# Layer 0's scores and values as 64x64 quadrant matmuls in turns, and one scatter with each step

## The chip, the cores and the metric

The kernel runs on one core of a Trainium2 chip. The metric is the device time of the whole program in microseconds (us); the kernel before takes 2517.85 us (median of 3 runs, 2517.65 to 2518.61). Times of single instructions come from one profiled execution of the same program, which took 2627.8 us.

## What is computed

Eight images of 256 channels and 1024 pixels go through two layers, all in fp32. Only layer 0 is touched by the larger part of the change, and the dispatch of layer 1's experts by the smaller part:

```python
# layer 0, per image: 8 heads of 64
qkv  = xt @ w_qkv + b_qkv
attn = softmax(einsum('bihd,bjhd->bijh', q, k) * 64**-0.5, axis=1)   # over the queries i
res  = einsum('bijh,bjhd->bihd', attn, v) @ w_out + b_out + xt
# layer 1, per image
t = t + attention(layer_norm(t))              # one head of width 256
t = t + moe(layer_norm(t))                    # 8 experts, the best 2 of each token
```

The softmax of layer 0 runs over the queries, so the sum that a score is divided by belongs to a key. The kernel folds it into the values.

## The kernel before, in words

The images go through `layer0` (L369), `attend` (L518), `normed` (L684) one after the other. Of seven images the tokens are scattered by expert to a table in DRAM (`dispatch`, L697), and one pass of `experts` (L867) works on them all; the eighth image goes through `dense`.

In `layer0` the heads are taken in pairs g (four pairs) and the keys in blocks j of 128 (eight blocks), so there are 32 steps (g, j) for an image and 256 in all. The queries and keys of a head pair lie as two times 64 partitions in `q` and `k`. One step does this:

- `score(at, h, n)` (L384): for head h = 0 or 1 and half n of the 1024 queries, a matmul with 64 rows (the width of a head) and 128 columns (the keys of the block), 512 queries long: psc. Head 0 uses the upper 64 rows of the array and head 1 the lower 64, so two of them can run at once. A score tile psc of one head fills two PSUM banks, and three such tiles exist (`ps_big`).
- `first_max` (L397) and `soften` (L406): VectorE takes the largest score of the first half (L401), then of the second half together with the first (L413); ScalarE writes the exponentials `ex` and their sum (L423); VectorE divides the values by the sum (L430, L432): `vs`.
- `gather_values(at)` (L439), which lags two steps behind (`LAG`): for each half n of the queries and each head h, a matmul with all 128 rows (the keys) and 64 columns (the width of the head), 512 queries long, added up in `po[n]` over the eight blocks. Head 0 uses columns 0 to 63 and head 1 columns 64 to 127, so again two can run at once.

The loop at L461 writes the order down by hand: score (at, head 0, first half), score (at-1, head 1, second half), `soften` of head 1, score (at, head 0, second half), score (at, head 1, first half), `soften` of head 0, and then the values of step at-2. In two steps of each of the first three head pairs a projection of the next pair follows (`project`, L292; 4 matmuls on the full array: pqk). With each step the generator `routing`, which is `dispatch` of the image before, is moved on to its next `yield` (L489). `dispatch` has 16 such places; behind the last of them it issues all 16 scatters (8 token blocks by 2 choices, L763) at one go. The tile framework's scheduler then places the instructions in five queues, one for each engine, and joins them by semaphores.

A matmul in fp32 is two instructions here, so the profile counts twice as many as the code writes; this text calls each of the two a pass.

Of the kernel before, what the change touches and what calls it, by code (L numbers as in the profile page):

```python
# [11 lines left out]
I32 = mybir.dt.int32  # L12
AF = mybir.ActivationFunctionType
ALU = mybir.AluOpType
AX = mybir.AxisListType


@with_exitstack
def kernel(
# [23 lines left out]
    nc = tc.nc  # L43
    P = 128
# [3 lines left out]
    DK = 64  # L48
    SCALE = DK ** (-0.5)
    NCC = C // P  # L50
    NT = S // P
    NH2 = S // 512
# [15 lines left out]
    small = ctx.enter_context(tc.tile_pool(name="small", bufs=6))  # L68
# [300 lines left out]
    def layer0(b, xT, begun, routing):  # L369

        v, qks = begun.v, begun.qks
        array = None
        res = one.tile([P, NPAIR, S], F32, tag="res", name=f"res_{b}")
        steps = [(g, j) for g in range(NPAIR) for j in range(NT)]
        LAG = 2
        seconds = {}  # L380
        pss, firsts, nmaxes, exps, sums, vss = {}, {}, {}, {}, {}, {}
        po = None

        def score(at, h, n):  # L384
            g, j = steps[at]
            q, k = qks[g]
            if n == 0:
                pss[at, h] = big(f"psc_{b}_{g}_{j}_{h}")
            r = slice(h * DK, (h + 1) * DK)
            mm = nc.tensor.matmul(  # L390
                pss[at, h][:, ts(n, 512)], k[r, ts(j, P)], q[r, ts(n, 512)], start=True, stop=True
            )
            if n == 1:

                tc.declare_no_dep(mm.ins, firsts.pop((at, h)).ins, reason="the other bank")

        def first_max(at, h):  # L397

            g, j = steps[at]
            nmax = small.tile([P, 1], F32, tag="nmax1", name=f"nmax1_{b}_{g}_{j}_{h}")  # L400
            firsts[at, h] = nc.vector.tensor_reduce(  # L401
                nmax, pss[at, h][:, ts(0, 512)], AX.X, ALU.max, negate=True
            )
            nmaxes[at, h] = nmax

        def soften(at, h):  # L406

            g, j = steps[at]
            ps = pss.pop((at, h))
            if h == 0:  # L410
                sums[at] = small.tile([P, 2], F32, tag="sums", name=f"sums_{b}_{g}_{j}")
            nmax = small.tile([P, 1], F32, tag="nmax", name=f"nmax_{b}_{g}_{j}_{h}")
            seconds[h] = nc.vector.tensor_scalar(  # L413
                scrap,
                ps[:, ts(1, 512)],
                -1.0,
                nmaxes.pop((at, h)),
                ALU.mult,
                ALU.min,
                accum_out=nmax,  # L420
            )
            ex = expp.tile([P, 1024], F32, tag="exps", name=f"ex_{b}_{g}_{j}_{h}")
            nc.scalar.activation(  # L423
                ex, ps, AF.Exp, bias=nmax, scale=1.0, accum_out=sums[at][:, h : h + 1]
            )
            exps[at, h] = ex
            if h == 1:

                rs = small.tile([P, 2], F32, tag="rs", name=f"rs_{b}_{g}_{j}")
                nc.vector.reciprocal(rs, sums.pop(at))  # L430
                vs = four.tile([P, 2, DK], F32, tag="vs", name=f"vs_{b}_{g}_{j}")
                nc.vector.tensor_mul(  # L432
                    vs,
                    v[:, j, ts(g, P)].rearrange("p (h d) -> p h d", d=DK),
                    rs.unsqueeze(2).to_broadcast([P, 2, DK]),
                )
                vss[at] = vs

        def gather_values(at):  # L439
            nonlocal po  # L440
            g, j = steps[at]
            if j == 0:
                po = [acc(f"po_{b}_{g}_{n}") for n in range(NH2)]
            vs = vss.pop(at)
            exs = [exps.pop((at, h)) for h in range(2)]
            for n in range(NH2):
                for h in range(2):
                    mm = nc.tensor.matmul(  # L448
                        po[n][h * DK : (h + 1) * DK, :],
                        vs[:, h, :],  # L450
                        exs[h][:, ts(n, 512)],
                        start=(j == 0),
                        stop=(j == NT - 1),
                    )
            if j == NT - 1:
                for n in range(NH2):
                    nc.scalar.copy(res[:, g, ts(n, 512)], po[n])
            return mm

        last = len(steps) - 1  # L460
        for at in range(last + LAG + 1):  # L461
            if at <= last:
                score(at, 0, 0)
            if 0 < at <= last + 1:
                score(at - 1, 1, 1)
                soften(at - 1, 1)
            if at <= last:

                with tc.issue_after(seconds[1].ins) if 1 in seconds else nullcontext():
                    first_max(at, 0)  # L470
                score(at, 0, 1)
                score(at, 1, 0)
                soften(at, 0)
                with tc.issue_after(seconds[0].ins):
                    first_max(at, 1)
            if at == 0:
                begun.rest()
                next(routing, None)
            if at >= LAG:
                array = gather_values(at - LAG)  # L480
            if at <= last:
                g, j = steps[at]
                if g + 1 < NPAIR and j in (3, 5):
                    if j == 3:
                        qks.append([])
                    qks[g + 1].append(project(b, xT, g + 1, len(qks[g + 1])))
                if array is not None:
                    with tc.issue_after(firsts[at, 1].ins), tc.issue_after(array.ins):
                        next(routing, None)  # L489
        for _ in routing:  # L490
            pass


        t1 = one.tile([P, NT, C], F32, tag="t1", name=f"t1_{b}")
        n = 1024 // C
        for i in range(0, NT, n):
            pt = big(f"pt_x_{b}_{i}")
            for j in range(n):
                for cc in range(NCC):
                    nc.tensor.transpose(  # L500
                        pt[:, j * C + cc * P : j * C + (cc + 1) * P], xT[:, cc, ts(i + j, P)], ident
                    )
            nc.vector.tensor_add(
                t1[:, i : i + n, :],
                pt.rearrange("p (j c) -> p j c", c=C),
                b_o.unsqueeze(1).to_broadcast([P, n, C]),
            )
        for i in range(NT):
            pr = acc(f"pr_{b}_{i}")
            for g in range(NPAIR):  # L510
                nc.tensor.matmul(  # L511
                    pr[:, :C], res[:, g, ts(i, P)], wo[:, g, :], start=(g == 0), stop=(g == NPAIR - 1)
                )
            nc.vector.tensor_add(t1[:, i, :], pr[:, :C], t1[:, i, :])
        return t1
# [181 lines left out]
    def dispatch(b, n2, l, group):  # L697

        gate, hots = yield from gates(b, l)
# [40 lines left out]
        group.counts = counts  # L740

        kept = []
        for k in range(2):
            yield
            hot = hots[k]
            sel = tmp("d_sel")
            nc.vector.tensor_mul(sel, hot, rows)
            row = keep.tile([P, NT], F32, tag=f"row{k}", name=f"row{k}_{b}")
            nc.vector.tensor_reduce(row, sel, AX.X, ALU.add)
            nc.vector.tensor_mul(sel, hot, e_iota.unsqueeze(1).to_broadcast([P, NT, E]))  # L750
            exp = keep.tile([P, NT], F32, tag=f"exp{k}", name=f"exp{k}_{b}")
            nc.vector.tensor_reduce(exp, sel, AX.X, ALU.add)
            yield
            to = small.tile([P, NT], F32, tag="d_to", name=f"d_to_{b}_{k}", bufs=2)
            nc.vector.scalar_tensor_tensor(to, exp, float(group.cap), row, ALU.mult, ALU.add)
            at = small.tile([P, NT], I32, tag="d_at", name=f"d_at_{b}_{k}", bufs=2)
            nc.vector.tensor_copy(at, to)  # L757
            kept.append((row, exp, at))
        for i in range(NT):
            for k in range(2):  # L760
                at = kept[k][2]
                view = group.views[2 * (NT * group.items.index(b) + i) + k]
                nc.gpsimd.indirect_dma_start(  # L763
                    out=view[:, :],
                    out_offset=bass.IndirectOffsetOnAxis(ap=at[:, i : i + 1], axis=0),
                    in_=n2[:, i, :],
                    in_offset=None,
                )
        group.kept[b] = gate, [(row, exp) for row, exp, _ in kept]

    def plan(group):

# [443 lines left out]
```

## Time and profile before

| what | value | where it is read |
|---|---|---|
| device time | 2517.85 us | the times |
| profiled execution | 2627.8 us, clock 0.979 | span and granted clock of the core |
| score passes psc (L390) | 2048, 553.3 us busy | groups of instructions |
| value passes po (L448) | 2048, 495.9 us busy | groups of instructions |
| VectorE per step: L413 and L401, two each | 750 and 679 ns | groups of instructions |
| ScalarE per step: L423, two | 1114 ns | groups of instructions |
| scatters (L763) | 112, 975 ns each on GpSimd | groups of instructions |

Busy time of PE counts a stretch once even where several passes run in it, so 2048 passes of mean 622 ns make 553.3 us. The chain that ended last is followed back from the last instruction; a share of it is time in which that line held up the end. `PE L390 <- ACT L423` after an idle time says that the matmul queue went on when that ScalarE instruction was done.

### The profile page before, as it was taken

Reading aid. Unit: us, or ns where it says so; the run is one execution under the profiler, and the core shown is the slowest. Engines: PE = TensorE matmul, PEld = TensorE weight load, DVE = VectorE, ACT = ScalarE, POOL = GpSimd, SP = SyncE. Lnnn points to the kernel's source line nnn. Section 1 sums busy time; section 2 is a strip of 40 time slices with the busy share of each in tenths; the row PEclk is TensorE's granted clock in tenths of the full one; section 3 lists DMA queues with packets and bytes.
Section 4 is the critical chain, followed back from the end, with each engine's and each line's share of the span. In section 5 each row is a group of like instructions: output and inputs, shape, how many; then the busy total and the mean of one; then the engine's idle time right before and its main releaser. Section 6 shows DMA issues by size and latency. Waiting matters only on the chain.

```text
span 2627.8 us, 27548 instructions
## 1 busy us (share of the span) xinstructions
PE 2504.9 (95%) x9919; PEld 1311.3 (50%) x9919; DVE 1538.1 (59%) x3738; ACT 891.0 (34%) x1491; POOL 386.0 (15%) x383
## 2 busy tenths in 40 slices
PE   9999989998999989998999899989998999997798
PEld 3346434643365336532563256324643488884566
DVE  5764766466656765576557664766476753334443
ACT  3541345134512542244214431444144422221212
POOL 0000020002000100002000200020002144435561
PEclk9999999999999999999999999999999999998899
DMA  7991000000000000000000000000000156663352
GB/s 289 385 333 44 32 33 17 1 17 33 1 17 17 19 15 17 16 1 33 17 17 1 32 17 0 17 32 1 0 17 33 53 196 225 214 196 100 104 166 103
DMA packets 82513, 187.61 MB, mean 71 GB/s; under 512 B 13992, under 2 KB 23880, under 8 KB 80584
## 3 DMA queue, kind: packets, MB, share of 16 engines
q1 hardware_dynamic: 57368, 118.65, 12.6%
q0 software_dynamic: 25008, 67.20, 8.2%
q8 instruction: 78, 1.28, 0.2%
q14 instruction: 59, 0.48, 0.1%
HBM read 100.49 MB, written 110.90 MB: 80 GB/s over the span
## 4 chain that ended last, share of the span: by engine, by line
PE 88%; DVE 3%; another core or an unknown queue 3%; issue 2%; DMA 2%; ACT 2%; SPq 0%; ACTq 0%; POOL 0%; DVEq 0%; POOLq 0%
PE psc L390 19%; PE po L448 17%; PE pqk L299 9%; PE py L571 8%; PE ps L545 7%; PE pr L511 4%; PE pv L335 4%; PE ph L903 3%; PE pe L928 3%; PE pdy L1110 2%; PE pdh L1086 2%; PE px L530 2%; PE pa L564 2%; PE pt_n L232 1%
## 5 line engine op out<-in xcount | busy, mean ns | idle before, releaser
L423 ACT ACTIVATE ex<-psc,nmax 128x1024 f32<-128x1024 f32 x512 | 570.5, 1114 | 639.5 <-DVE scrap L413 576.2
L390 PE MATMUL psc<-qk,qk 64*128 64x512 f32 x2048 | 553.3, 622 | 12.6 <-ACT ex L423 8.1
L413 DVE TENSOR_SCALAR_CACHE_REDUCE scrap<-psc,nmax 128x512 f32<-128x512 f32 x512 | 384.2, 750 | 229.7 <-PE psc L390 137.4
L448 PE MATMUL po<-ex,vs 128*64 128x512 f32 x2048 | 495.9, 605 | 2.1 <-DVE nmax L401 2.1
L390 PEld LDWEIGHTS psc<-qk,qk 64*128 64x128 f32 x2048 | 209.8, 185 | 337.7 <-ACT ex L423 176.1
L401 DVE TENSOR_REDUCE nmax<-psc 128x1 f32<-128x512 f32 x512 | 347.4, 679 | 16.6 <-PE psc L390 16.0
L299 PE MATMUL pqk<-xT,wqkv 128*128 128x512 f32 x512 | 249.8, 633 | 53.8 <-ACT ex L423 53.8
L448 PEld LDWEIGHTS po<-ex,vs 128*64 128x64 f32 x2048 | 124.8, 136 | 337.7 <-issue 212.5
L571 PE MATMUL py<-n,aT 128*128 128x256 f32 x1024 | 244.4, 393 | 16.7 <-DVE aT L566 11.9
L571 PEld LDWEIGHTS py<-n,aT 128*128 128x128 f32 x1024 | 196.0, 195 | 81.9 <-DVE aT L566 49.7
L545 PE MATMUL ps<-nT,xa 128*128 128x512 f32 x512 | 236.5, 592 | 0.0
L692 POOL TENSOR_TENSOR t<-t,n 128x2048 f32<-128x2048 f32 x8 | 36.3, 4537 | 1280.2 <-issue 1004.4
L299 PEld LDWEIGHTS pqk<-xT,wqkv 128*128 128x128 f32 x512 | 99.1, 201 | 195.8 <-issue 102.6
L763 POOL DMA_INDIRECT rows<-n,d_at x112 | 109.2, 975 | 593.3 <-DVE d_at L757 561.3
L556 ACT ACTIVATE ex<-ps,nmax 128x1024 f32<-128x1024 f32 x64 | 71.3, 1115 | 352.2 <-DVE nmax L553 321.9
L576 DVE SCALAR_TENSOR_TENSOR t<-py,rs,t 128x256 f32<-128x256 f32 x64 | 31.0, 484 | 232.6 <-PE py L571 201.7
L289 DVE TENSOR_SCALAR qk<-pqk,b_qk 128x512 f32<-128x512 f32 x100 | 75.1, 751 | 121.4 <-PE pqk L299 121.4
L545 PEld LDWEIGHTS ps<-nT,xa 128*128 128x128 f32 x512 | 93.6, 190 | 79.9 <-issue 73.7
L975 POOL DMA_INDIRECT yk<-y,yat x112 | 112.4, 1003 | 122.1 <-DVE o L1007 71.8
L335 PE MATMUL pv<-wqkv,xT 128*128 128x512 f32 x256 | 119.6, 596 | 1.0 <-ACT wqkv L105 1.0
L553 DVE TENSOR_REDUCE nmax<-ps 128x1 f32<-128x1024 f32 x64 | 78.3, 1224 | 59.1 <-PE ps L545 54.1
L511 PE MATMUL pr<-wo,res 128*128 128x256 f32 x512 | 111.8, 379 | 0.0
(191 smaller groups left out, 2426.9 us busy)
## 6 DMA issues: line engine op xcount, KB each, us to landing
rows<-wb SPq DMA_DIRECT2D x7, 8192.0 KB
y<-yb SPq DMA_DIRECT2D x63, 256.0 KB
xT<-in_x_dram SPq DMA_DIRECT2D x7, 1024.0 KB
sums<-t SPq DMA_DIRECT2D x7, 1024.0 KB
o<-sums SPq DMA_DIRECT2D x7, 1024.0 KB
out_dram<-oT SPq DMA_DIRECT2D x14, 512.0 KB
wpack<-in_L_ffn_w_dram SPq DMA_DIRECT2D x4, 1024.0 KB
wb<-in_L_ffn_w_dram SPq DMA_DIRECT2D x16, 256.0 KB
```

What stands on the lines that cost most here:

```text
L299: mm = nc.tensor.matmul(pq[:, ts(n, 512)], wqkv[:, cc, t, ts(g, P)], xT[:, cc, ts(n, 512)], start=(cc == 0), stop=(cc == NCC - 1),)
L335: nc.tensor.matmul(pv, self.xT[:, cc, ts(i, P)], wqkv[:, cc, 2, :], start=(cc == 0), stop=(cc == NCC - 1),)
L390: mm = nc.tensor.matmul(pss[at, h][:, ts(n, 512)], k[r, ts(j, P)], q[r, ts(n, 512)], start=True, stop=True)
L401: firsts[at, h] = nc.vector.tensor_reduce(nmax, pss[at, h][:, ts(0, 512)], AX.X, ALU.max, negate=True)
L413: seconds[h] = nc.vector.tensor_scalar(scrap, ps[:, ts(1, 512)], -1.0, nmaxes.pop((at, h)), ALU.mult, ALU.min, accum_out=nmax,)
L423: nc.scalar.activation(ex, ps, AF.Exp, bias=nmax, scale=1.0, accum_out=sums[at][:, h : h + 1])
L448: mm = nc.tensor.matmul(po[n][h * DK : (h + 1) * DK, :], vs[:, h, :], exs[h][:, ts(n, 512)], start=(j == 0), stop=(j == NT - 1),)
L511: nc.tensor.matmul(pr[:, :C], res[:, g, ts(i, P)], wo[:, g, :], start=(g == 0), stop=(g == NPAIR - 1))
L545: nc.tensor.matmul(psc[:, ts(n, 512)], xa[:, ec, ts(i, P)], nT[:, ec, ts(n, 512)], start=(ec == 0), stop=(ec == NCC - 1),)
L571: nc.tensor.matmul(py[:, :D], aT[:, ts(m, P)], n1[:, m, :], start=(m == 0), stop=(m == NT - 1))
L763: nc.gpsimd.indirect_dma_start(out=view[:, :], out_offset=bass.IndirectOffsetOnAxis(ap=at[:, i : i + 1], axis=0), in_=n2[:, i, :], in_offs ...
L975: nc.gpsimd.indirect_dma_start(out=yk[:, i, k, :], out_offset=None, in_=self.group.y[:, :], in_offset=bass.IndirectOffsetOnAxis(ap=ats[k][ ...
```

## The change

Every score matmul becomes two, each for 64 of the 128 keys, so it uses 64 rows and 64 columns: one quadrant of the array. Every value matmul becomes two, each for 64 of the 128 keys, so it too uses 64 rows and 64 columns. With that all of a step's matmuls, but for the projections, have one shape, and the work of scores and values can share the array. [...] The values of a step are therefore done in two turns, one after the first scores of a step and one at the old place: in turn 0 the upper 64 keys write bank `po[0]` and the lower 64 keys `po[1]`, in turn 1 the other way round. Each half of a turn (2 matmuls, one for each head) waits for an empty instruction on another engine, the relay, which itself waits for the matmuls of an earlier half. The relay's queue is GpSimd's for image 0 and the DMA queue's engine (SyncE) for the others.

The scatters come one by one, each with its own one-column index tile and a `yield` behind it, so that one is issued with each step.

```diff
-            mm = nc.tensor.matmul(
-                pss[at, h][:, ts(n, 512)], k[r, ts(j, P)], q[r, ts(n, 512)], start=True, stop=True
-            )
+            for c in range(2):
+                mm = nc.tensor.matmul(
+                    pss[at, h][ts(c, DK), ts(n, 512)],
+                    k[r, j * P + c * DK : j * P + (c + 1) * DK],
+                    q[r, ts(n, 512)],
...
+        relay = nc.gpsimd if b == 0 else nc.sync
...
+        def gather_values(at, turn):
...
-            for n in range(NH2):
+            for half in range(2):
+                keys = ts(half, DK)
+                n = (half + turn) % 2
                 for h in range(2):
                     mm = nc.tensor.matmul(
-                        po[n][h * DK : (h + 1) * DK, :],
-                        vs[:, h, :],
-                        exs[h][:, ts(n, 512)],
-                        start=(j == 0),
-                        stop=(j == NT - 1),
+                        po[n][ts(h, DK), :],
+                        vss[at][keys, h, :],
+                        exps[at, h][keys, ts(n, 512)],
+                        start=(j == 0 and turn == 0),
+                        stop=(j == NT - 1 and turn == 1),
                     )
+                    if h == 0 and (j > 0 or turn > 0):
+                        tc.add_manual_dep(mm.ins, turned[1 - half].ins.name, BEHIND)
+
+                turned[half] = relay.nop()
+                tc.add_manual_dep(turned[half].ins, mm.ins.name, BEHIND)
...
             if 0 < at <= last + 1:
                 score(at - 1, 1, 1)
                 soften(at - 1, 1)
+            if at >= LAG:
+                gather_values(at - LAG, 0)
...
             if at >= LAG:
-                array = gather_values(at - LAG)
+                array = gather_values(at - LAG, 1)
...
-        for i in range(NT):
-            for k in range(2):
-                at = kept[k][2]
+        for k in range(2):
+            for i in range(NT):
+                at = small.tile([P, 1], I32, tag="d_at", name=f"d_at_{b}_{i}_{k}", bufs=4)
+                nc.vector.tensor_copy(at, tos[k][:, i : i + 1])
...
                 nc.gpsimd.indirect_dma_start(
                     out=view[:, :],
-                    out_offset=bass.IndirectOffsetOnAxis(ap=at[:, i : i + 1], axis=0),
+                    out_offset=bass.IndirectOffsetOnAxis(ap=at, axis=0),
                     in_=n2[:, i, :],
                     in_offset=None,
                 )
+                yield
```

More of the change, by code (lines that the diff above doesn't have):

```diff
@@ L15 @@
 AX = mybir.AxisListType
+BEHIND = mybir.DependencyInfo(mybir.DependencyClass.Sync, mybir.DependencyReason.DATA)
 @with_exitstack
@@ L379, in layer0 @@
         LAG = 2
-        seconds = {}
+        seconds, turned = {}, {}
+        relay = nc.gpsimd if b == 0 else nc.sync
         pss, firsts, nmaxes, exps, sums, vss = {}, {}, {}, {}, {}, {}
@@ L389, in score @@
             r = slice(h * DK, (h + 1) * DK)
-            mm = nc.tensor.matmul(
-                pss[at, h][:, ts(n, 512)], k[r, ts(j, P)], q[r, ts(n, 512)], start=True, stop=True
-            )
-            if n == 1:
-                tc.declare_no_dep(mm.ins, firsts.pop((at, h)).ins, reason="the other bank")
+            for c in range(2):
[3 more added lines that the diff above has]
+                    q[r, ts(n, 512)],
+                    start=True,
+                    stop=True,
+                )
+                if n == 1:
+                    tc.declare_no_dep(mm.ins, firsts[at, h].ins, reason="the other bank")
         def first_max(at, h):
@@ L437, in soften @@
                 vss[at] = vs
-        def gather_values(at):
+        def gather_values(at, turn):
             nonlocal po
             g, j = steps[at]
-            if j == 0:
+            if j == 0 and turn == 0:
                 po = [acc(f"po_{b}_{g}_{n}") for n in range(NH2)]
-            vs = vss.pop(at)
-            exs = [exps.pop((at, h)) for h in range(2)]
-            for n in range(NH2):
+            for half in range(2):
+                keys = ts(half, DK)
+                n = (half + turn) % 2
                 for h in range(2):
                     mm = nc.tensor.matmul(
-                        po[n][h * DK : (h + 1) * DK, :],
-                        vs[:, h, :],
-                        exs[h][:, ts(n, 512)],
-                        start=(j == 0),
-                        stop=(j == NT - 1),
-                    )
+                        po[n][ts(h, DK), :],
[3 more added lines that the diff above has]
+                        stop=(j == NT - 1 and turn == 1),
+                    )
+                    if h == 0 and (j > 0 or turn > 0):
+                        tc.add_manual_dep(mm.ins, turned[1 - half].ins.name, BEHIND)
+                turned[half] = relay.nop()
+                tc.add_manual_dep(turned[half].ins, mm.ins.name, BEHIND)
+            if turn == 0:
+                return mm
+            vss.pop(at)
+            for h in range(2):
+                exps.pop((at, h))
             if j == NT - 1:
@@ L742, in dispatch @@
         kept = []
+        tos = []
         for k in range(2):
@@ L755, in dispatch @@
             nc.vector.scalar_tensor_tensor(to, exp, float(group.cap), row, ALU.mult, ALU.add)
-            at = small.tile([P, NT], I32, tag="d_at", name=f"d_at_{b}_{k}", bufs=2)
-            nc.vector.tensor_copy(at, to)
-            kept.append((row, exp, at))
-        for i in range(NT):
-            for k in range(2):
-                at = kept[k][2]
+            kept.append((row, exp))
+            tos.append(to)
+            group.kept[b] = gate, kept
+        for k in range(2):
+            for i in range(NT):
+                at = small.tile([P, 1], I32, tag="d_at", name=f"d_at_{b}_{i}_{k}", bufs=4)
+                nc.vector.tensor_copy(at, tos[k][:, i : i + 1])
                 view = group.views[2 * (NT * group.items.index(b) + i) + k]
@@ L768, in dispatch @@
                 )
-        group.kept[b] = gate, [(row, exp) for row, exp, _ in kept]
+                yield
     def plan(group):
```

## The prediction, made before the changed kernel ran

> **What bounds the kernel now.** I read the page's busy shares first, then the chain that ended last, then one step of layer 0 in the timeline.
>
> ```profile
> PE 2504.9 (95%) x9919; PEld 1311.3 (50%) x9919; DVE 1538.1 (59%) x3738; ACT 891.0 (34%) x1491; POOL 386.0 (15%) x383
> ...
> PE psc L390 19%; PE po L448 17%; PE pqk L299 9%; PE py L571 8%; PE ps L545 7%; PE pr L511 4%; PE pv L335 4%; PE ph L903 3%; PE pe L928 3%; PE pdy L1110 2%; PE pdh L1086 2%; PE px L530 2%; PE pa L564 2%; PE pt_n L232 1%
> ```
>
> PE is the bound, and 36% of the chain is the two lines that change. The chain in order of time shows that they alternate and nothing else comes between them:
>
> ```profile
> 407.59 1.99 PE psc L390 x8
> 409.58 1.87 PE po L448 x8
> 411.45 1.97 PE psc L390 x8
> 413.42 1.87 PE po L448 x8
> ```
>
> A step is 1.98 + 1.87 = 3.85 us. Inside one step (start, duration):
>
> ```profile
> 411.38 0.30 PEld L390 LDWEIGHTS psc<-qk,qk 64*128 64x128 f32 x4 [0.81 <-ACT ex L423]
> ...
> 411.91 0.19 PEld L390 LDWEIGHTS psc<-qk,qk 64*128 64x128 f32 x1 [0.23 <-issue]
> ...
> 412.56 0.75 DVE L413 TENSOR_SCALAR_CACHE_REDUCE scrap<-psc,nmax 128x512 f32<-128x512 f32 x1 [0.75 <-PE psc L390]
> ...
> 413.35 0.20 PEld L448 LDWEIGHTS po<-ex,vs 128*64 128x64 f32 x4 [0.76 <-DVE scrap L413]
> ...
> 413.83 0.14 PEld L448 LDWEIGHTS po<-ex,vs 128*64 128x64 f32 x2 [0.29 <-issue]
> ...
> 414.26 0.14 PEld L448 LDWEIGHTS po<-ex,vs 128*64 128x64 f32 x2 [0.28 <-issue]
> ...
> 415.21 0.30 PEld L390 LDWEIGHTS psc<-qk,qk 64*128 64x128 f32 x4 [0.81 <-ACT ex L423]
> ```
>
> A slot holds two passes at once, and a new slot starts when its weight loads do: 413.83 to 414.26 is 0.43 us. Eight slots would be 8 x 0.43 = 3.44 us; the step has 3.85. The missing 0.41 lies at the two changes of shape: the first values slot is 0.48 long, the first score slot 0.53 (411.38 to 411.91), and each phase's last slot 0.1 to 0.15 longer than 0.43.
>
> **What the Trainium skill says.** "TensorEngine Tiling (Array Packing)", Tiling Modes, Key Properties: changing the tiling mode drains TensorE. The trace agrees: 0.41 us a step, as above. The same page, Restrictions and Gotchas, Gotcha 1: row tiles may not access one PSUM bank at the same time and software must see to it. No run here shows that yet; it is what the relay is for. "TensorE: Matmul & The Clock Gate", Part 3, The mechanism: matmuls on different tiles run together, each a few ns behind the other. The router's four column tiles agree: 16 passes in 1.07 us, where 16 in a row at the 0.215 us between two passes of L511 (equally 256 columns) would be 3.4 us.
>
> ```profile
> 284.91 1.07 PE L599 MATMUL pl<-n2T,rT 128*32 128x256 f32 x16
> ```
>
> **The change, part by part.**
>
> *One shape.* 8 matmuls of 2 passes become 16 of 2 passes a step, 8 passes on each quadrant. If four run at once that is again 8 slots, 3.44 us, and the 0.41 us of drains goes. This is the most the idea can give: 0.41 x about 200 steps without projection = 82 us.
>
> *The relays.* In the built order of the changed kernel a step's values are four halves: turn 0 upper, turn 0 lower, turn 1 upper, turn 1 lower. The code looks up `turned[1 - half]` after the other half has just overwritten it, so turn 0 lower waits for turn 0 upper although they write different banks; the count that each half waits for goes up by exactly one from half to half. Every half therefore waits for the half just before it. Data alone would need only every second of these waits. Behind the waiting weight load, in the same queue, stand all later scores; who waits for those is VectorE.
>
> The length H of one link, from the half's first weight load to the next half's:
> - first pass to second pass 0.48 (413.35 to 413.83, the same 64 columns);
> - start of the last pass to the start of a waiting engine 0.64 (a slot starts at 411.91; VectorE, which had idled 0.75 for it, starts at 412.56);
> - the relay itself about 0.02 (a bare wait on GpSimd, row below, 0.017 at the median);
> - the relay's release to the weight load 0.05 (the score load at 412.29 follows the end of ScalarE's read, 412.05 + 0.19, by 0.05).
>
> ```profile
> L763 POOLq EVENT_SEMAPHORE x17: 17/17/43, 281.0 to 2002.0; - x17
> ```
>
> H = 1.19 us. I take no less than 1.12 (a quicker reaction than VectorE's) and no more than 1.30 (0.05 more for each of the two hops). Four links are 4.76 us, more than the 3.44 of the slots, so the chain of relays sets the step, and the scores run beside it: when an upper half ends after 0.91, the upper quadrants have one score matmul (0.86) queued and then idle until the chain returns. VectorE's work a step is 2 x 0.68 + 2 x 0.68 + about 0.4 = 3.1 us and ScalarE's 2 x 1.3 = 2.6, both under 4.76.
>
> Per image, against before:
> - 23 steps without projection: 4.76 - 3.845 = 0.915 each, 21.0 us.
> - 6 steps with one. Before: 3.845 + 3.62 = 7.47. After, the built order has the projection's first matmul between the third and fourth half and the rest behind the fourth, so there are four changes of shape. A pass in a new shape starts 0.53 after the last one of the old. From the first half's load: 2H to the third half; 0.48 + 0.53 for it; 0.53 + 0.53 for two projection passes; 0.48 + 0.53 for the fourth half; 0.53 + 4 x 0.43 + 0.53 for six; then 0.86 because the next half queues behind a score matmul on its quadrant. 2 x 1.19 + 6.72 = 9.10; 1.63 each, 9.8 us.
> - The end of an image, with values alone: the last two intervals are 2.92 and 2.84 before, 4.76 each after, +3.8; the last step's values 3H + 1.07 = 4.64 instead of 1.94, +2.7.
> - The first step of a head pair waits for no relay in turn 0 but for two ScalarE copies of 0.59, about as long: 0.
>
> Sum 21.0 + 9.8 + 3.8 + 2.7 = 37.3 us; times 8 images, 298 us.
>
> *The scatters.* In the profile the 16 scatters do harm: VectorE gets its release from PE late.
>
> ```profile
> 920.31 0.28 DVE L432 TENSOR_TENSOR vs<-v,rs 128x128 f32<-128x128 f32 x1
> 930.17 0.75 DVE L413 TENSOR_SCALAR_CACHE_REDUCE scrap<-psc,nmax 128x512 f32<-128x512 f32 x1 [9.57 <-remote]
> ```
>
> There are seven such gaps, one in each image that scatters. From first score pass to last value pass image 0, which scatters nothing, takes 152.3 us, the others 162.1 to 169.4, together 96 us more, of which 6 is the added count matmul. But the profiled execution is 2627.8 - 2517.85 = 110 us longer than the timed one, and I see no other place for so much. So I take it that the gaps belong to the profiled execution and spreading the scatters gives the timed one nothing; the other bound is 85 us. The 14 more small casts an image (171 ns each at L757, 2.4 us) fall into VectorE's free 1.6 us a step. The last scatter now comes at the end of the image's steps; what waits for it is the next write of `n` (the layer norm of `attend`, after some 15 us of L511) and, in the last image, the first expert rows, behind the same 15 us. 0.
>
> Sum: 2517.85 + 298 = 2816, said as 2815.
>
> **The rivals.**
> - *The waits are hidden and the drains go* (faster). If the halves bind only where data demands, two links (2.4 us) fit under 3.44: -0.40 x 25 x 8 = -80, and +0.7 x 48 for the additional changes of shape at projections = +34: 2472, or 2390 if the scatters' gaps exist without a profile. For it: that the trace shows concurrent tiles at full rate. Against: the counts of the waits. 6%, a sixth of it within 0.2%.
> - *Quadrants run in pairs only*: 16 slots, 6.9 us a step, +3 x 250: about 3270. For it: before, never more than two passes with 64 rows or 64 columns share a slot. Against: L599's four. 5%.
> - *The relay is slow*: H = 1.5, since no trace here shows a wait on SyncE that answers PE; +0.31 x 115 links x 8 = +285: 3100. 9%.
>
> **How the numbers follow.** The forecast has 80%. Its spread: 115 links an image (23 x 4 + 6 x 2 + 2 x 4 + 3), so 920 x -0.07 = -64 and 920 x 0.11 = +101; and up to -85 if the timed run had the gaps, which I give one in four. 2690 to 2930 takes that in and leaves the rivals out, which have 20%. Faster by 0.2%: 0.05; within 0.2%: 0.01; slower: 0.94.
>
> **What would show it.** In the profile after: four groups of value passes a step, 1.19 us apart; a step of about 4.8 us; PE's weight loads at the value line waiting for GpSimd or SyncE; score passes at the same time as value passes; a slot still 0.43 us; no 9 us gap in VectorE. A value group that starts before the one before it has ended, or a step under 3.85, breaks the forecast; a slot longer than 0.43 makes the second rival; a link over 1.3 the third.

## The result and the profile after

The changed kernel takes 2831.23 us (median of 4 runs, 2830.76 to 2832.50), the kernel before beside it 2518.17 us: a ratio of 1.1244, 95% interval 1.1225 to 1.1264. It is slower by 313 us; 297 had been forecast.

The page of the changed kernel, its busy shares and its chain that ended last by line:

```profile
PE 2781.0 (98%) x14015; PEld 1425.1 (50%) x14015; DVE 1575.8 (56%) x3836; ACT 890.1 (31%) x1491; POOL 387.6 (14%) x383
...
PE po L459 21%; PE psc L395 14%; PE py L594 7%; PE pqk L300 7%; PE ps L568 6%; PE pr L534 3%; PE ph L929 3%; PE pe L954 3%; PE pv L336 3%; ACT ex L432 2%; PE pdy L1136 2%; PE pdh L1112 2%; PE px L553 2%; PE pa L587 2%; DVE scrap L422 1%; PE pt_n L233 1%
```

PE's share is 98%, where it was 95% in the profile that the prediction was made from and 99% in a second profile of the kernel before (below). So the share says nothing about the loss: "busy" counts a PE in which one quadrant of four works. What grew in the chain is the value line, from 19% of 2514 us in that second profile to 21% of 2829.

One step of the changed kernel in the timeline (start, duration; L459 are the values, L395 the scores):

```profile
421.85 1.09 PE L395 MATMUL psc<-qk,qk 64*64 64x512 f32 x8
...
423.88 0.14 PEld L459 LDWEIGHTS po<-ex,vs 64*64 64x64 f32 x2
423.88 0.65 PE L459 MATMUL po<-ex,vs 64*64 64x512 f32 x2
423.90 0.13 PEld L395 LDWEIGHTS psc<-qk,qk 64*64 64x64 f32 x1
423.90 0.74 PE L395 MATMUL psc<-qk,qk 64*64 64x512 f32 x2
...
424.37 0.60 PE L459 MATMUL po<-ex,vs 64*64 64x512 f32 x2
...
425.06 0.20 PEld L459 LDWEIGHTS po<-ex,vs 64*64 64x64 f32 x4
...
426.24 0.14 PEld L459 LDWEIGHTS po<-ex,vs 64*64 64x64 f32 x2
```

Eight score passes on four quadrants take 1.09 us, where one matmul of two passes on one quadrant takes 0.48 + 0.59: four quadrants do run at once. The value groups begin at 423.88, 425.06 and 426.24, 1.18 us apart, and scores run beside them. From first pass to first pass the four links of a step are 1.18, 1.27, 1.17 and 1.18 us; the step is 4.79 us, or 4.75 behind a projection, where it was 3.845. In image 0, whose relay is on GpSimd, it is 4.85. Inside a link: 0.49 from first to second pass, 0.69 from the second pass to the next half's load.

The relays, the empty instructions of L469, and who waited for them:

```profile
L469 SPq EVENT_SEMAPHORE  x863: 17/17/28, 336.7 to 2321.1; - x173
L469 POOLq EVENT_SEMAPHORE  x124: 17/17/43, 38.0 to 219.6; - x124
...
  PEld po L459: 37.6, 181
```

The waits come to only 37.6 us in this view, because time in which any quadrant still works isn't counted as idle. This is why the wait has to be read from the distance of the groups and not from the list of waits.

From first score to last value an image takes 192.4 us (192.55 in image 0, 204.41 in image 1, 194.47 in image 7), where an undisturbed execution of the kernel before takes 153.3 (152.26 to 156.69). Over eight images that is 1553.5 - 1230.1 = 323 us more, and the rest of the program is 8 us shorter (0.9 in each of the seven stretches between the images, and 2 behind the last): 315 us, the difference of the two spans.

### The profile page after: what moved, and what is told of

The parts are those of the page before. It is cut to its first block, busy times and chain, and to the rows that moved or that the text cites. A ratio compares the mean times of both kernels' runs of the same rounds, so it can differ in the third digit from the quotient of the medians.

```text
span 2829.1 us, 36869 instructions
## 1 busy us (share of the span) xinstructions
PE 2781.0 (98%) x14015; PEld 1425.1 (50%) x14015; DVE 1575.8 (56%) x3836; ACT 890.1 (31%) x1491; POOL 387.6 (14%) x383
## 3 DMA queue, kind: packets, MB, share of 16 engines
q1 hardware_dynamic: 57368, 118.65, 11.6%
## 4 chain that ended last, share of the span: by engine, by line
PE 79%; DVE 4%; ACT 3%; DMA 1%; issue 1%; ACTq 0%; POOL 0%; SPq 0%; POOLq 0%; DVEq 0%
PE po L459 21%; PE psc L395 14%; PE py L594 7%; PE pqk L300 7%; PE ps L568 6%; PE pr L534 3%; PE ph L929 3%; PE pe L954 3%; PE pv L336 3%; ACT ex L432 2%; PE pdy L1136 2%; PE pdh L1112 2%; PE px L553 2%; PE pa L587 2%; DVE scrap L422 1%; PE pt_n L233 1%
## 5 line engine op out<-in xcount | busy, mean ns | idle before, releaser
L459 PE MATMUL po<-ex,vs 64*64 64x512 f32 x4096 | 1081.7, 611 | 8.3 <-ACT res L478 7.6
L395 PE MATMUL psc<-qk,qk 64*64 64x512 f32 x4096 | 1038.7, 598 | 6.8 <-ACT ex L432 6.6
L395 PEld LDWEIGHTS psc<-qk,qk 64*64 64x64 f32 x4096 | 329.5, 132 | 540.6 <-issue 470.8
L459 PEld LDWEIGHTS po<-ex,vs 64*64 64x64 f32 x4096 | 210.4, 131 | 250.1 <-issue 87.4
L594 PEld LDWEIGHTS py<-n,aT 128*128 128x128 f32 x1024 | 192.4, 192 | 68.5 <-DVE aT L589 43.7
L300 PEld LDWEIGHTS pqk<-xT,wqkv 128*128 128x128 f32 x512 | 89.3, 189 | 148.8 <-issue 109.1
L439 DVE RECIPROCAL rs<-sums 128x2 f32<-128x2 f32 x256 | 42.4, 166 | 183.5 <-ACT ex L432 183.5
```

Of the source, the lines that this page charges most:

```text
L300: mm = nc.tensor.matmul(pq[:, ts(n, 512)], wqkv[:, cc, t, ts(g, P)], xT[:, cc, ts(n, 512)], start=(cc == 0), stop=(cc == NCC - 1),)
L395: mm = nc.tensor.matmul(pss[at, h][ts(c, DK), ts(n, 512)], k[r, j * P + c * DK : j * P + (c + 1) * DK], q[r, ts(n, 512)], start=True, stop ...
L459: mm = nc.tensor.matmul(po[n][ts(h, DK), :], vss[at][keys, h, :], exps[at, h][keys, ts(n, 512)], start=(j == 0 and turn == 0), stop=(j == ...
L594: nc.tensor.matmul(py[:, :D], aT[:, ts(m, P)], n1[:, m, :], start=(m == 0), stop=(m == NT - 1))
```

## The experiments

The waits by bank, the scatters alone, the quadrants without the scatters and the second hop ran together, beside 17 runs of the kernel before (median 2515.25 us). The second profile of the kernel before, the scores alone and VectorE's order ran together (before: 2516.47), the last experiment by itself (before: 2514.36).

### Waits by bank

```diff
-                        tc.add_manual_dep(mm.ins, turned[1 - half].ins.name, BEHIND)
+                        tc.add_manual_dep(mm.ins, turned[n].ins.name, BEHIND)
-                turned[half] = relay.nop()
-                tc.add_manual_dep(turned[half].ins, mm.ins.name, BEHIND)
+                turned[n] = relay.nop()
+                tc.add_manual_dep(turned[n].ins, mm.ins.name, BEHIND)
```

> The changed kernel, but each half of the values waits for the last half that wrote its own bank instead of for the half just before it (turned is looked up by bank). Matmuls, shapes and relays are the same ones. My theory (the chain of four links of 1.19 us sets the step): two links of 1.19 now fit under the eight slots of 0.43 us, so the chain lets go and the step falls from 4.76 to between the slots' 3.44 and VectorE's own 3.5 a step (two times 0.75 + 0.08 + 0.69, and 0.46 for the values): about 3.5 to 3.6, some 50 us an image less than now, 2430 to 2480 us in all and no wait of PE for the relay inside a step. Rival (the quadrants themselves cost, by changes of mode or by running in pairs): the step stays at 4.7 or so and the time within 1% of 2831. Second rival (the relay answers late whatever the order): a step of 3.8 or more, 2550 or more.

Measured: 2617.58 us (2615.41 to 2620.32), ratio to before 1.0406 (1.0390 to 1.0422). With the same matmuls and the same relays, 214 us of the 313 are gone. So it is which half waits for which, not the quadrants, that cost them. It need not all be time spent waiting: with the new waits the scheduler also placed PE's matmuls differently. In the changed kernel a projection is split in two by a half of the values (2 passes, then 6), and at the end of an image transposes stand between the halves; here the projection's 8 passes stand together, and most halves at the end too. How much of the 214 us is due to this placement was not tried; by the prediction's own 0.7 us for the extra changes of shape, 48 projections make an estimate of about 34 us. But the time is not the 2430 to 2480 that I expected. Steps behind a projection do reach 3.43 us; steps in a row take 3.98. In the chain that ended last VectorE and ScalarE have a larger share now (4% and 3% in the changed kernel):

```profile
PE 62%; DVE 14%; ACT 8%; issue 2%; DMA 2%; ACTq 0%; POOL 0%; SPq 0%; POOLq 0%; DVEq 0%
```

One such step in the timeline, VectorE and ScalarE alone (in brackets the idle time before and what ended it):

```profile
108.79 0.19 ACT L432 ACTIVATION_READ_ACCUMULATOR ex<-psc,nmax 128x1 f32 x1
109.01 0.17 DVE L439 RECIPROCAL rs<-sums 128x2 f32<-128x2 f32 x1 [0.73 <-ACT ex L432]
...
109.21 0.29 DVE L441 TENSOR_TENSOR vs<-v,rs 128x128 f32<-128x128 f32 x1
109.42 0.74 DVE L422 TENSOR_SCALAR_CACHE_REDUCE scrap<-psc,nmax 128x512 f32<-128x512 f32 x1
...
110.09 0.69 DVE L410 TENSOR_REDUCE nmax<-psc 128x1 f32<-128x512 f32 x1
...
110.90 0.75 DVE L422 TENSOR_SCALAR_CACHE_REDUCE scrap<-psc,nmax 128x512 f32<-128x512 f32 x1
...
111.75 1.11 ACT L432 ACTIVATE ex<-psc,nmax 128x1024 f32<-128x1024 f32 x1 [0.28 <-DVE scrap L422]
112.76 0.19 ACT L432 ACTIVATION_READ_ACCUMULATOR ex<-psc,nmax 128x1 f32 x1
```

It is a closed loop: ScalarE's sum (108.79), the reciprocal, the scaled values, three reductions, the exponential, and the next sum at 112.76, 3.97 us later. VectorE stands idle 0.73 us in it, because the scheduler placed the reciprocal directly behind the wait for the sum. In the kernel before the reciprocal stands behind the next second-half reduction (L413, then L430), and VectorE doesn't wait for the sum.

### The scatters alone

The kernel before with the changed end of `dispatch`: the part of the diff from `tos = []` on, and nothing else.

> The kernel before with the scatter part of the change alone: one scatter with each step, each with its own small cast; scores and values as before. My theory (the 9 us gaps of VectorE belong to the profiled execution): the timed run stays within 0.3% of 2518, and the profiled execution, 110 us longer than the timed one before, loses some 90 of these. Rival (the gaps are in every execution): the timed run falls to about 2433.

Measured: 2516.48 us (2513.39 to 2520.15, 13 runs), ratio 1.0002 (0.9994 to 1.0010). The scatter part is worth nothing in the timed runs, within 0.1%. The profiled execution took 2516.51 us, without the 110 us more, but this doesn't show that spreading the scatters removed them, as the second profile of the kernel before will show.

### The quadrants without the scatters

The changed kernel with the end of `dispatch` of the kernel before.

> The changed kernel without its scatter part: quadrants and relays as in the change, the 16 scatters of an image at one go as before. My theory: the timed run stays within 0.5% of 2831, and the profiled execution is some 90 us or more longer than the timed one again. Rival (the gaps are in every execution): about 2915 timed.

Measured: 2834.33 us (2831.82 to 2837.99), ratio 1.1265 (1.1247 to 1.1282). All of the loss lies in the quadrants and relays. The second half of my expectation missed: the profiled execution is 2835.07 us, no longer than the others, though all 16 scatters go at once in it.

### The kernel before, profiled again

> The kernel before, unchanged, profiled once more. If the seven gaps of 9 us in VectorE belong to every profiled execution of this kernel, the profile shows them again and its execution is about 110 us longer than 2515. If they belonged to that one execution, the span is 2515 and an image that scatters takes about 153 us.

Measured: 2515.74 us for the profiled execution, a span of 2514.0. An image that scatters takes 153.3 us, and VectorE passes through the 16 scatters (L763) undisturbed. Two lines each of VectorE's and GpSimd's timeline:

```profile
898.90 0.69 DVE L401 TENSOR_REDUCE nmax<-psc 128x1 f32<-128x512 f32 x1
899.71 0.75 DVE L413 TENSOR_SCALAR_CACHE_REDUCE scrap<-psc,nmax 128x512 f32<-128x512 f32 x1
```

```profile
897.98 0.97 POOL L763 DMA_INDIRECT rows<-n,d_at  x1 [0.30 <-issue]
899.25 0.97 POOL L763 DMA_INDIRECT rows<-n,d_at  x1 [0.30 <-issue]
```

The seven gaps (6.9 to 9.6 us long) belonged to one execution of the kernel before, the one whose profile the prediction was made from. They belong neither to the kernel nor to every profiled execution of it. Compared with the second profile, the first is 114 us longer: 84 of these lie in layer 0 of the seven images that scatter, 30 behind the last image. In layer 0 each gap comes with a stretch of 7 to 10 us in which the granted clock was 0.5 (61 us in all, none in the second profile).

### A second hop in each link

```diff
+        hop = None if b == 0 else nc.gpsimd
...
                 tc.add_manual_dep(turned[half].ins, mm.ins.name, BEHIND)
+                if hop:
+                    first = turned[half]
+                    turned[half] = hop.nop()
+                    tc.add_manual_dep(turned[half].ins, first.ins.name, BEHIND)
```

> The changed kernel with a second empty instruction behind each relay of images 1 to 7, on GpSimd, so that a link is PE to SyncE to GpSimd to PE instead of PE to SyncE to PE. Nothing else is added, and nothing waits for it but the next half. My theory (the chain of links sets the end): each of the 115 links an image grows by one hop of 0.05 to 0.10 us, 805 links, 40 to 80 us, and somewhat more where a scatter of about 1 us stands in GpSimd's queue: 2870 to 2960. Rival (something else than the chain sets the step, the relay being hidden): within 0.5% of 2831.

Measured: 2994.73 us (2983.11 to 2995.74), ratio 1.1886 (1.1865 to 1.1908); 163 us more than the changed kernel, and above the range that I gave. The undisturbed step grows from 4.79 to 4.99 us: 0.05 us for each of four links, so 805 links make 40 us. Most of the other 120 us come from GpSimd's queue. In most of the later steps of an image one link is 2.24 to 2.25 us instead of 1.23, since a scatter stands ahead of the hop and itself waits for VectorE's cast of its indices. By an estimate some 29 us of the 120 come with a lower clock: at the end of images 1, 2 and 5 the granted clock was 0.5 for 20.5 us, and images 2 and 5 take 222.6 us where images 3 and 4, which have no such stretch, take 213.1. What brought it on is open. The waits of this kernel between 700 and 860 us (us in total, times, longest):

```profile
POOL rows L794 <- DVE d_at L792: 178.3, 14, 106.9
...
PEld po L460 <- POOLq L474: 27.5, 72, 1.7
```

That a relay's instruction without any work moves the end by its own length and by what is queued ahead of it shows that the chain of links sets the time of the changed kernel. It also shows that SyncE, whose queue holds hardly anything else there, was a better place for it than GpSimd.

### The scores alone as quadrants

The kernel before with the changed `score` (two matmuls of 64 keys each), and nothing else.

> The kernel before with the scores alone as quadrants: two matmuls of 64 keys for each one of 128; values, scatters and order as before, no relay. My theory (the quadrants themselves cost nothing, four run in the time of two halves; the cost of the change is the chain of relays): within 0.5% of 2515. Rival (quadrants run in pairs or cost in their number): a step longer by up to 1.7 us, 2700 to 2950.

Measured: 2506.83 us (2505.87 to 2508.45), ratio 0.9965 (0.9951 to 0.9979). Twice as many score matmuls cost nothing; they even give 9.6 us. The first of the score slots in the weight loads of this kernel:

```profile
405.39 0.21 PEld L391 LDWEIGHTS psc<-qk,qk 64*64 64x64 f32 x8 [0.81 <-ACT ex L428]
405.87 0.14 PEld L391 LDWEIGHTS psc<-qk,qk 64*64 64x64 f32 x2 [0.28 <-issue]
```

It is 0.48 us long instead of 0.53: the first weights of a shape, now 64 columns wide, are loaded in 0.21 us and not 0.30. The step is 3.82 us, and an image some 1.0 us shorter. Scores and values still have two shapes here (64x64 and 128x64), and the step stays well above eight slots, 3.44 us.

### Waits by bank, with VectorE's order put back

The code of the first experiment, with the reciprocal and the scaled values taken out of `soften` into a `fold`, which is placed behind the second-half reduction of the next step:

```diff
-            if h == 1:
-                rs = small.tile([P, 2], F32, tag="rs", name=f"rs_{b}_{g}_{j}")
...
+        def fold(at):
+            rs = small.tile([P, 2], F32, tag="rs", name=f"rs_{b}_{g}_{j}")
...
                 with tc.issue_after(seconds[0].ins):
+                    if at > 0:
+                        fold(at - 1)
                     first_max(at, 1)
```

> The kernel with the waits by bank, and VectorE's order of the kernel before put back by hand: the reciprocal of the sums and the scaled values (0.17 and 0.29 us) of a step come behind the next step's second largest score of head 0, instead of ahead of it, where VectorE stood idle 0.73 us for ScalarE's sum. My theory (with the waits by bank, what holds a step at 3.98 us is a loop through VectorE and ScalarE: sum, reciprocal, values, three reductions, exponentials): the loop goes, VectorE's 3.5 us of work a step is then the bound, beside the slots' 3.44, and the time is 2470 to 2530. Rival (the step of 3.98 comes from PE, from the quadrants or from a late relay): within 0.5% of 2617.

Measured: 2507.44 us (2506.15 to 2512.54), ratio 0.9969 (0.9959 to 0.9979). PE's passes start in the order of the first experiment, but for swaps by one or two places between passes that run at once, and 110 us go. So VectorE's order, and the loop through ScalarE that it closes, was what held that kernel. Part of the 110 us is a lower clock: in the first experiment the granted clock was 0.5 for 54 us of layer 0, in stretches of 3.4 and 6.8 us; here for none. Of images 2 to 6 of the first experiment the one without such a stretch takes 161.8 us, the two with 6.8 us of them 165.2, the two with 10.2 us 166.3. So each costs about half its length, an estimate of 27 of the 110 us. It fits that PE pauses less now (3.4 to 3.9 us in most images, where it was 7.4), but the image without a stretch has the same pauses as the others, so what lowers the clock stays open. The step is 3.66 us now, and in the timeline the values wait for the scaled values:

```profile
622.12 0.28 DVE L442 TENSOR_TENSOR vs<-v,rs 128x128 f32<-128x128 f32 x1
...
622.46 0.21 PEld L460 LDWEIGHTS po<-ex,vs 64*64 64x64 f32 x8 [0.88 <-DVE vs L442]
```

### The scaled values one reduction earlier

```diff
-                with tc.issue_after(seconds[0].ins):
-                    if at > 0:
-                        fold(at - 1)
+                behind = seconds[0]
+                if at > 0:
+                    with tc.issue_after(behind.ins):
+                        behind = fold(at - 1)
+                with tc.issue_after(behind.ins):
                     first_max(at, 1)
```

> The kernel with the waits by bank and VectorE's order put back, and in addition the scaled values of a step ahead of the next largest-score reduction instead of behind it (0.67 us earlier). In the step of 3.66 us of the kernel without this, the first values of a step wait some 0.9 us for these scaled values. My theory (that wait is what keeps the step above the slots' 3.44): a step of 3.5 to 3.6, 2480 to 2503. Rival (VectorE's and ScalarE's own work of 3.5 us and its waits hold the step, and the reduction that now comes later delays the exponentials): 2507 or more.

Measured: 2491.60 us (2490.91 to 2493.39), ratio 0.9909 (0.9892 to 0.9925). This beats both kernels, by 23 us and by 340. The time lies in my range, the step below it, for the 3.5 us of VectorE's work that I counted in three expectations were too much: VectorE is busy for 3.16 us of a step of 3.44 here. PE's weight loads in the last head pair of an image:

```profile
675.65 0.39 PEld L395 LDWEIGHTS psc<-qk,qk 64*64 64x64 f32 x8 [0.47 <-ACT ex L432]
676.28 0.62 PEld L461 LDWEIGHTS po<-ex,vs 64*64 64x64 f32 x8 [0.23 <-DVE vs L442]
677.00 0.77 PEld L395 LDWEIGHTS psc<-qk,qk 64*64 64x64 f32 x8
677.88 0.73 PEld L461 LDWEIGHTS po<-ex,vs 64*64 64x64 f32 x8
679.09 0.39 PEld L395 LDWEIGHTS psc<-qk,qk 64*64 64x64 f32 x8 [0.47 <-ACT ex L432]
```

From 675.65 to 679.09 is a step of 3.44 us, eight slots of 0.43 without a drain, with all relays in place. An image takes 149.2 us instead of 153.3.

## Why the prediction was right, and where its sum was off

**The direction and the mechanism** were right. The waits by bank take 214 us back with the same matmuls and relays, and a longer relay makes the step longer by its own length. Both say that the chain of links, each half waiting for the half just before it, sets the step.

**One link.** Forecast 1.19 us, measured 1.17 to 1.18, and 1.27 for one of the four. The sum of the four is 4.79 for 4.76. Of the working, the part between the last pass and the next load was 0.71 and measured 0.69.

**A step with a projection.** Forecast 9.10, measured 9.09, and 10.01 where the count matmul comes in. The four changes of shape were counted rightly.

**The head-pair boundary.** Forecast 0, measured 5.80 + 4.16 instead of 2 x 4.79: +0.38 for each of three boundaries, 9 us over eight images.

**The end of an image.** This term was mis-sized. For the last steps I took links of 1.19 us, as elsewhere. They are 1.37 there, since a transpose of the next image's input (pt_x, on the full array) stands between every two halves. Weight loads of the changed kernel at the end of image 2:

```profile
824.12 0.20 PEld L523 LDWEIGHTS pt_x<-ident,xT 128*128 128x128 f32 x2 [0.81 <-issue]
824.49 0.19 PEld L459 LDWEIGHTS po<-ex,vs 64*64 64x64 f32 x4 [0.17 <-SPq L469]
825.50 0.20 PEld L523 LDWEIGHTS pt_x<-ident,xT 128*128 128x128 f32 x2 [0.81 <-issue]
825.86 0.20 PEld L459 LDWEIGHTS po<-ex,vs 64*64 64x64 f32 x4 [0.17 <-issue]
```

The last three intervals and the rest took 9.65 us more than before, where the forecast (3.8 + 2.7, and one step of 0.9) has 7.4: 2.2 an image, 18 us in all.

**The start of an image** was not in the sum. The first values come 10.03 us after the first scores instead of 11.6, since turn 0 stands ahead of the second scores: -1.6 an image, -13 us.

**Image 1** was not in the sum. It takes 12 us more than images 2 to 6. In its first step the second turn of values comes 22.9 us after the first scores and not 11.8, behind two more steps of scores and a projection, and ScalarE waits for a free `exps` buffer meanwhile:

```profile
350.68 1.11 ACT L432 ACTIVATE ex<-psc,nmax 128x1024 f32<-128x1024 f32 x1 [8.85 <-PE po L459]
```

SyncE waited for PE here (12.7 us at the longest) and not the other way, so the cause is where the scheduler put this turn in PE's queue. Why it put it there, in the first image whose relay is on SyncE, I did not try; that stays open.

The sum closes: 298 + 18 + 9 - 13 + 12 - 8 (the rest of the program) = 316, and the spans differ by 315. That 297 came so near to 313 is luck in part: the terms that I mis-sized or left out are 39 us one way and 21 the other.

**The scatters.** Forecast 0, and the scatters alone give 1.0002 in the ratio. The reason was only half right. I held that the gaps belonged to the profiled execution, and the timed runs show no sign of them. But a second profile of the same kernel has none, nor has that of the quadrants with the scatters at one go. So the gaps were not the harm of 16 scatters under a profile but a disturbance of that one execution, and its cause is open. I also saw no other place for its 110 us, though 30 lie behind the last image. I gave one chance in four to 85 us in the timed runs; a second profile would have settled it.

**The rivals.** "Quadrants run in pairs only" falls with eight passes in 1.09 us and with the scores alone at 0.9965. "The relay is slow" falls with links of 1.18. "The waits are hidden and the drains go" was worked out at 2472. For the kernel as it was changed it falls, since its waits bind; with waits by bank the drains do go, but 2472 missed something: when PE needs 3.44 us a step, VectorE's order decides. With the order that the scheduler chose the time is 2617.58, with a better one 2491.60. The Trainium skill's statement that a change of the tiling mode drains TensorE ("TensorEngine Tiling (Array Packing)", Tiling Modes, Key Properties) agrees with this last kernel: scores and values in one shape take 3.44 us a step, in two shapes 3.845, or 3.82 with the scores alone as quadrants.

## What to carry to other kernels

When two operations are kept apart by a wait through another engine, price the whole loop (pass, pass, release, relay, load: 1.18 us here) and count how many of them lie in a row; then ask which of these waits the data demand, since here half of them were an accident of a lookup behind an overwrite, and taking them out gave 214 us. The empty relay belongs on a queue in which nothing waits for anything else. When the bound engine gets faster, look at the order of the next one before calling the gain real: a reciprocal placed too early held a step at 3.98 us instead of 3.66.

## What the runs showed of the hardware that I had not expected

- A relay over an idle engine costs little: 0.05 us for a second hop, and 0.69 us from the start of the last pass (itself 0.59 to 0.60 long) to the next half's weight load. Most of a link is the matmul it waits for.
- Doubling the number of score matmuls by halving their columns made the kernel 0.35% faster (0.9951 to 0.9979). The first load of a shape takes 0.21 us with 64 columns and 0.30 with 128, and the first slot is shorter by 0.05 us.
- The order of VectorE's work can reach PE's clock: with the waits by bank the granted clock was 0.5 for 54 us of layer 0, with VectorE's order put back for none. Every run shows it: the mean granted clock is 0.983 to 0.985 in the four of the first, 0.993 to 0.995 in the nine of the second.
- One execution was longer by 110 us than all others of its kernel, with gaps of 6.9 to 9.6 us that look like a reason. Its own time (2627.8 beside 2517.85) was the first sign, its mean granted clock (0.979, where 0.995 is usual here) another.
